# The third corner's sum moves from VectorE to TensorE, and one scan product from GpSimd to VectorE

## The chip, the cores and the metric

The kernel runs on one core of a Trainium2 chip. The core has TensorE (PE: matmuls and transposes, with its weight loads shown apart as PEld), VectorE (DVE), ScalarE (ACT), GpSimd (POOL) and the DMA queues, of which SP issues most and POOL issues the indirect ones. Each engine works through its own instructions in order; the engines wait for one another by semaphores. The metric is the device time of one execution in microseconds (us), lower is better.

## The reference, cut to what matters

Four layers run one after another on a (4, 128, 128, 128) tensor, each as `x = x + layer(groupnorm(x))`. Layer 0 is a deformable 3x3 convolution: an ordinary convolution gives each output pixel and each of nine taps an offset and a mask, the input is sampled there between its four neighbours, and the samples are projected by the weights.

```python
return corner(y0i, x0i, (1 - ly) * (1 - lx)) + corner(y0i, x0i + 1, (1 - ly) * lx) + corner(y0i + 1, x0i, ly * (1 - lx)) + corner(y0i + 1, x0i + 1, ly * lx)
...
sampled = _bilinear_sample(x, py, px) * mask[:, None]
return jnp.einsum('bckhw,ock->bohw', sampled, weight.reshape(weight.shape[0], C, KK))
```

Layer 1 is a dilated 5x7 convolution with two small projections. Layer 2 is a state-space block: after projections and a depthwise convolution, a scan with 16 states for each of 128 channels runs over the 16,384 pixels in four directions,

```python
h = h * dA + (d * u)[..., None] * b[:, :, None, :]
y = jnp.einsum('bkcn,bkn->bkc', h, c)
```

and a norm, a gate and a projection follow. Layer 3 is a 3x3 convolution with an edge term. The edit concerns the sum of the four corners in layer 0 and the products `h * c` of layer 2.

## The kernel before, in words

**Order.** The scan of layer 2 is the main line: `scan` goes through 4 images x 4 directions x 32 pieces = 512 blocks `t` of 512 pixels. All other work (the layers before and after the scan, for the images next and before) is woven in by generators: after every scan instruction `scan` yields the share of its work that is done, and `together` pulls the side work until its own share has caught up. `keep_order` at the end holds each engine to the order in which the instructions were recorded, so nothing is moved by a scheduler: an instruction that waits holds back all that stands behind it on its engine. Layer 0 of image 0 runs before the scan begins; those of images 1 to 3 run beside the scan of the image before.

**A scan block** handles 2048 rows (128 channels x 16 states) in four groups `g` of four 128x512 pieces `ng`. For each group DVE multiplies the inputs by `b` (L946, 128x2048, one factor read from PSUM); ACT makes the decays in PSUM (L875); DVE runs four scans (L989, 1.27 us each); ACT copies the last column of two pieces out as the next block's start (`carry_on`, L909); then `outputs` multiplies those two pieces in place by `c` (L915, 128x1024, both factors in SBUF): half 0 after the second scan, half 1 in the group after. PE adds the rows up with a gather matrix (`sums`, L889). A block so has eight products. While layer 0 is beside the scan (`beside["busy"] == "POOL"`, so `on_vector`), half 1's four run on DVE and half 0's four on POOL; elsewhere all are on POOL, and with `busy == "PE"` POOL also adds two pieces (L917), which saves PE a matmul. The lines around the third scan of a group:

```python
if ng == 2 and before[0] >= 0 and on_vector:
    outputs(*before, 1, nc.vector)
if ng == 2:
    carry_on(t, g, 0)
    outputs(t, g, 0)
```

**Layer 0** does 288 iterations `n` an image: 32 blocks of four rows x nine taps. `gather` (L419) issues four indirect DMAs from POOL, each of which brings, for 128 pixels, the four neighbours (128 channels each) side by side into `g`, [128, 4 rows, 4 neighbours, 128], a ring of four buffers. `weigh_low` (L433) scales neighbours 0, 1 and 2 on ACT, 128x128 at a time: neighbour 0 into the PSUM tile `pw` (bank 2), 1 and 2 in place in `g`. `weigh` on DVE adds 1 and 2 onto `pw` (L445, two 128x512 adds) and then multiplies neighbour 3 by its weight and adds `pw` in one instruction for each row (L448), which gives `v`. `turn` transposes the four rows of `v` on PE into the PSUM tile `pst` (bank 1, L456); `copy` brings it to SBUF on ACT (L460); `project` multiplies it by the tap's weights on PE (L466), which add up in bank 0 over nine taps; `add` (L473, L474) finishes a block on DVE. `positions` (from L341) makes the next strip's indices and weights in small pieces between. The iterations are laid over each other by `weave`, each step with its lag in iterations:

```python
order = [[(2, weigh_low(1)), (3, turn)], [(5, add), (0, gather), (2, weigh_low(2))],
         [(2, weigh_low(0))], [(3, copy), (0, look)], [(2, weigh), (4, project)]]
```

So in one round of the loop ACT weighs iteration n, PE turns n - 1 (whose `v` DVE made at the end of the round before), ACT copies it, DVE weighs n, PE projects n - 2, and POOL gathers n + 2. The gather takes over the buffer of four iterations before.

Of the kernel before, what the change touches and what calls it, by code (L numbers as in the profile page):

```python
# [18 lines left out]
P = 128  # L19
# [12 lines left out]
NG = 4  # L32
# [78 lines left out]
def conv_preact_kernel(ctx: ExitStack, tc: tile.TileContext, a: dict, nb: int):  # L111
    nc = tc.nc
# [11 lines left out]
    def load(pool, src, shape, name, **kw):  # L124
        t = pool.tile(shape, F32, name=name, **kw)
        nc.sync.dma_start(t, src)
        return t

    def bank(which, name):
        return psb.tile([P, N], F32, name=name, tag=f"bank{which}")  # L130
# [23 lines left out]
    ident = const.tile([P, P], F32, name="ident")  # L154
# [29 lines left out]
    for k in range(NDIR):  # L184
        pw = bank(0, "pwd")
# [8 lines left out]
    def blk(t, i):  # L194
        return t[:, i * N : (i + 1) * N]
# [99 lines left out]
    def layer0(st):  # L295
# [3 lines left out]
        with ExitStack() as s:  # L299
# [30 lines left out]
            got = {}  # L330
# [76 lines left out]
            def where(n):  # L407
                i, k = divmod(n, KK)
                return i, k, i // BPS, i % BPS
# [29 lines left out]

            def weigh(n):  # L440
                i, k, j, q = where(n)
                wv, g = got["i", j][0], got.pop(("g", n))
                pw = got.pop(("w", n)).rearrange("p (r c) -> p r c", r=R)
                for c in (1, 2):
                    nc.vector.tensor_add(pw, pw, g[:, :, c, :])  # L445
                got["v", n] = v = gp.tile([P, R, P], F32, name="v", bufs=2)
                for r in range(R):
                    nc.vector.scalar_tensor_tensor(  # L448
                        v[:, r, :], g[:, r, 3, :], wv[:, r, q, k, 3:4], pw[:, r, :], ALU.mult, ALU.add
                    )  # L450

            def turn(n):
                v = got.pop(("v", n))
                got["t", n] = pst = bank(1, "pst")
                for r in range(R):
                    nc.tensor.transpose(pst[:, r * P : (r + 1) * P], v[:, r, :], ident)  # L456

            def copy(n):
                got["c", n] = smp = pp.tile([P, N], F32, name="smp")
# [307 lines left out]
    def scan(pull):  # L767
# [11 lines left out]
        def decays(at):  # L779

            while ahead["made"] < min(at + (2 if beside.get("spare") else 1) + 1, len(seq) * NST):
                decay(ahead["made"])
                ahead["made"] += 1

        def fetch(t):
            if t < len(seq):
                st, k, i, _ = seq[t]
                while st.get("out", 0) < (i + 1 if k == 0 else NBLK + 1):
                    pull()
                    tick()  # L790
                if "y" not in st:
                    st["y"] = image("yrow"), image("ycol")
                us = st["u"]
                if not stored(us[0]):
                    flush()
                blocks[t]["u"] = load(sp, blk(us[k % 2], i), [P, N], "u", bufs=2)
# [47 lines left out]
        def spread_steps(t, g):  # L844

            blocks[t]["p", g] = p = sp.tile([P, 2, N], F32, name="spread", bufs=3)
            src = blocks[t]["steps"][g * Q : (g + 1) * Q]
            nc.sync.dma_start(
                p.rearrange("p j t -> p (j t)"), src.unsqueeze(1).to_broadcast([Q, P // Q, 2 * N])
            )  # L850
# [6 lines left out]
        def spread_states(t, what):  # L857

            blocks[t][what] = p = bp.tile([P, NG, N], F32, name=what)
            src = blocks[t]["bc"][("bb", "cb").index(what)].rearrange("(s n) t -> s (n t)", n=NG)  # L860
            nc.sync.dma_start(
                p.rearrange("p n t -> p (n t)"), src.unsqueeze(0).to_broadcast([Q, P // Q, NG * N])
            )
# [14 lines left out]
        def sums(t, g, half):  # L878

            c = blocks[t]  # L880
            second = seq[t][3]
            if g == 0 and half == 0:
                c["y"] = pss.tile([P, N], F32, name="yacc")
            last = g == NG - 1 and half == 1
            parts = (2 * half, 2 * half + 1)
            if half and c.get(("added", g)):
                parts = parts[:1]
            for ng in parts:
                nc.tensor.matmul(  # L889
                    c["y"], gather[:, g, :], c["h", g][:, ng, :],  # L890
                    start=g == 0 and ng == 0, stop=last and ng == parts[-1] and not second,
                )
            if last and second:
                nc.tensor.matmul(c["y"], ident, c["before"], start=False, stop=True)
# [9 lines left out]
        def carry_on(t, g, half):  # L904

            end = 0 if seq[t][3] else N - 1
            n = g * NG + 2 * half
            h = blocks[t]["h", g][:, 2 * half : 2 * half + 2, :]
            nc.scalar.copy(blocks[t]["carry"][:, n : n + 2].unsqueeze(2), h[:, :, end : end + 1])  # L909

        def outputs(t, g, half, engine=nc.gpsimd):

            c = blocks[t]
            h = c["h", g][:, 2 * half : 2 * half + 2, :]
            engine.tensor_mul(h, h, c["cb"][:, 2 * half : 2 * half + 2, :])  # L915
            if half and g % 2 and beside.get("busy") == "PE":
                engine.tensor_add(h[:, 0, :], h[:, 0, :], h[:, 1, :])  # L917
                c["added", g] = True
# [15 lines left out]
        for t, (st, k, i, back) in enumerate(seq):  # L934
            c = blocks[t]
            carry = c["carry"]
            more = prepare(t + 2) if t + 2 < len(seq) else iter(())
            if t > 0:
                fetch(t + 3)
            for g in range(NG):  # L940
                then = (t, g + 1) if g + 1 < NG else (t + 1, 0)
                soon = (t, g + 2) if g + 2 < NG else (t + 1, g + 2 - NG)
                before = (t, g - 1) if g else (t - 1, NG - 1)
                earlier = (t, g - 2) if g > 1 else (t - 1, g + NG - 2)
                c["h", g] = h = hp.tile([P, NG, N], F32, name="h")
                nc.vector.tensor_tensor(  # L946
                    h, c["pdu", g].unsqueeze(1).to_broadcast([P, NG, N]), c["bb"], ALU.mult
                )
                on_vector = beside.get("busy") == "POOL"
                if before[0] >= 0:  # L950
                    carry_on(*before, 1)
                    if not on_vector:
                        outputs(*before, 1)
                if soon[0] < len(seq):
                    spread_steps(*soon)
                at = t * NST + g * NG
                decays(at)
                if g == 1:
                    if t + 1 < len(seq):
                        spread_states(t + 1, "bb")  # L960
                if g == 2 and t + 1 < len(seq):
                    spread_states(t + 1, "cb")
                if g == 3 and back:
                    c["before"] = load(sp, blk(st["y"][k % 2], i), [P, N], "before")
                for ng in range(NG):
                    n = g * NG + ng
                    if ng == 1:
                        decays(at + 1)
                        if earlier[0] >= 0:
                            sums(*earlier, 1)  # L970
                    if ng == 2 and g == 1 and t > 0:
                        finish(t - 1)
                    if n % NST and ng != 2:
                        next(more, None)
                    if ng == 2 and before[0] >= 0 and on_vector:
                        outputs(*before, 1, nc.vector)
                    if ng == 2:
                        carry_on(t, g, 0)
                        outputs(t, g, 0)
                        decays(at + 2)  # L980
                        next(more, None)
                        if then[0] < len(seq):
                            inputs_up(*then)
                    if ng == 3 and before[0] >= 0:
                        sums(*before, 0)
                    o, f = h[:, ng, :], c["a", n]
                    if back:
                        o, f = o[:, ::-1], f[:, ::-1]
                    nc.vector.tensor_tensor_scan(o, f, o, carry[:, n : n + 1], ALU.mult, ALU.add)  # L989
                    if ng == 3:  # L990
                        decays(at + 3)
                    yield (t * NST + n + 1) / slots
            for _ in more:
                pass
        t = len(seq) - 1
# [396 lines left out]
```

## Time and profile before

| | |
|---|---|
| median of three runs | 22988.54 us (22963.23 to 22989.79) |
| the profiled execution's own time | 22958.5 us |
| its span, first to last instruction | 22956.7 us |
| mean granted TensorE clock | 0.872 |
| busy share of the span | PE 74%, DVE 82%, ACT 72%, POOL 75% |
| instructions | 176948 |

How to read it: a row of a group names the line, engine, operation, tiles (out<-in), shapes and count, then the busy time in us and the mean of one in ns, and then how long the engine had stood idle before such instructions and whose end released it ("issue": nothing that the profile shows). The table of stretches cuts the span by time and gives each engine's busy time in each. The granted clock is the share of full TensorE speed that the chip allowed. A busy engine is not by itself the bound; what counts is which wait ends last.

Four stretches have layer 0 in them, by the first and last gather: 236 to 2108 us, 3786 to 5873, 9486 to 11465 and 14824 to 16800. Most of the page's later slices show DVE at 8 or 9 tenths.

### The profile page before, as it was taken

The numbers are of one execution on the slowest core, as the hardware profiler recorded it, in microseconds if no ns is written. First come the engines' busy times: TensorE is split into PE (matmuls) and PEld (weight loads), VectorE is DVE, ScalarE is ACT, GpSimd is POOL, SyncE is SP. The second block draws the span as 40 slices with busy tenths as digits, with TensorE's granted clock in tenths as the row PEclk, the third lists the DMA queues.
The fourth block names the chain that finished last, engine by engine and source line by source line (L and its number), as shares of the span: only waits on it lengthen the run. The fifth ranks groups of instructions, "written<-read, shape, count | busy, mean of one in ns | idle before, by whom it ended". The sixth has DMA issues, their size and how long they took to land. (4 is left out here: it accounts for less than half of the span.)

```text
span 22956.7 us, 176948 instructions
## 1 busy us (share of the span) xinstructions
PE 16964.7 (74%) x38018; PEld 6618.0 (29%) x38018; DVE 18925.7 (82%) x19765; ACT 16485.0 (72%) x37282; POOL 17224.0 (75%) x11499
## 2 busy tenths in 40 slices
PE   3445886666878888766688887766688978788778
PEld 1112222222323333222233333322232333233223
DVE  3443489999998899889898899988898889999873
ACT  4665677888778766788868776688877867666553
POOL 3553477877788888777778788877778889877773
PEclk7667998887999999887799999987799999899889
DMA  7556468776766787777776687777776677555663
GB/s 214 175 176 182 150 204 286 249 236 227 249 204 210 216 242 258 237 238 239 240 243 203 205 251 243 248 235 244 238 254 204 206 214 231 188 196 199 194 182 111
DMA packets 2560065, 5005.19 MB, mean 218 GB/s; under 512 B 1059136, under 2 KB 1330952, under 8 KB 2416656
## 3 DMA queue, kind: packets, MB, share of 16 engines
q1 hardware_dynamic: 2190352, 3785.61, 50.8%
q0 software_dynamic: 368640, 1208.25, 17.2%
q8 instruction: 309, 5.06, 0.1%
q14 instruction: 764, 6.26, 0.1%
HBM read 4065.12 MB, written 857.74 MB: 214 GB/s over the span
## 5 line engine op out<-in xcount | busy, mean ns | idle before, releaser
L915 POOL TENSOR_TENSOR h<-h,cb 128x1024 f32<-128x1024 f32 x3740 | 8813.7, 2363 | 2826.7 <-ACT carry L909 2720.0
L989 DVE TENSOR_TENSOR_SCAN h<-pa,carry,h 128x512 f32<-128x512 f32 x8192 | 9981.1, 1267 | 277.7 <-ACT pa L875 184.0
L889 PE MATMUL yacc<-h,gather_sb 128*128 128x512 f32 x15258 | 8309.4, 675 | 1203.8 <-POOL h L915 610.9
L875 ACT ACTIVATE pa<-spread,neg_a 128x512 f32<-128x512 f32 x8192 | 5614.5, 686 | 3236.9 <-DVE h L989 3092.0
L419 POOL DMA_INDIRECT g<-table,idx x4608 | 4550.4, 988 | 2040.2 <-issue 1250.8
L946 DVE TENSOR_TENSOR h<-dub,bb 128x2048 f32<-128x2048 f32 x2048 | 4665.4, 2278 | 1297.3 <-issue 648.2
L889 PEld LDWEIGHTS yacc<-h,gather_sb 128*128 128x128 f32 x15258 | 3138.1, 217 | 5564.2 <-issue 3906.8
L456 PE MATMUL pst<-ident,v 128*128 128x128 f32 x4608 | 1193.7, 372 | 3102.3 <-DVE v L448 1666.8
L433 ACT ACTIVATE g<-g,wt 128x128 f32<-128x128 f32 x9216 | 2865.2, 389 | 171.4 <-DMA g<-table,idx 119.9
L445 DVE TENSOR_TENSOR pw<-pw,g 128x512 f32<-128x512 f32 x2304 | 1598.4, 694 | 1435.4 <-ACT pw L433 1191.6
L433 ACT ACTIVATE pw<-g,wt 128x128 f32<-128x128 f32 x4608 | 1694.9, 368 | 752.6 <-remote 298.4
L456 PEld LDWEIGHTS pst<-ident,v 128*128 128x128 f32 x4608 | 722.9, 160 | 4457.7 <-issue 2475.0
L466 PE MATMUL acc<-smp,w_sb 128*128 128x512 f32 x2304 | 1563.8, 768 | 118.7 <-DVE x L473 102.0
L448 DVE SCALAR_TENSOR_TENSOR v<-g,wt,pw 128x128 f32<-128x128 f32 x4608 | 1293.5, 342 | 114.4 <-issue 2.7
L909 ACT COPY carry<-h 128x2 f32<-128x2 f32 x4096 | 764.1, 187 | 704.2 <-DVE h L989 695.3
L855 ACT COPY dub<-spread 128x512 f32<-128x512 f32 x2048 | 1187.0, 580 | 57.3 <-DMA spread<-stepsd 19.9
L1207 PE MATMUL p<-xn,w_l_sb 128*128 128x508 f32 (+2 forms) x2304 | 1146.1, 616 | 1.8 <-ACT xn L1186 1.8
L808 PE MATMUL pdt<-u,wd 128*128 128x512 f32 x1024 | 593.4, 663 | 472.9 <-DVE h L946 431.7
L824 PE MATMUL pxbc<-u,xbc_sb 128*128 128x512 f32 x1024 | 584.8, 654 | 410.0 <-DVE h L946 406.0
L706 PE MATMUL px<-win,convw_sb 128*128 128x508 f32 (+1 forms) x1536 | 837.6, 627 | 4.7 <-DMA win<-win 4.7
L708 PE MATMUL py<-win,diag 128*64 128x508 f32 (+1 forms) x1536 | 837.0, 627 | 0.0
L460 ACT COPY smp<-pst 128x512 f32<-128x512 f32 x1152 | 664.6, 577 | 169.2 <-remote 157.1
(172 smaller groups left out, 17159.0 us busy)
## 6 DMA issues: line engine op xcount, KB each, us to landing
spread<-stepsd SPq DMA_DIRECT2D x2048, 512.0 KB
bb<-bcd SPq DMA_DIRECT2D x512, 1024.0 KB
cb<-bcd SPq DMA_DIRECT2D x512, 1024.0 KB
stepsd<-steps SPq DMA_DIRECT2D x512, 512.0 KB
table<-gt SPq DMA_DIRECT2D x512, 256.0 KB
g<-table,idx POOLq DMA_INDIRECT x4608
u<-urow SPq DMA_DIRECT2D x256, 256.0 KB
yrow<-y SPq DMA_DIRECT2D x256, 256.0 KB
```

What stands on the lines that cost most here:

```text
L419: nc.gpsimd.indirect_dma_start(out=g[:, r].rearrange("p q c -> p (q c)"), out_offset=None, in_=table, in_offset=bass.IndirectOffsetOnAxis( ...
L433: nc.scalar.activation(pw[:, r * P : (r + 1) * P] if c == 0 else g[:, r, c, :], g[:, r, c, :], AF.Copy, scale=wv[:, r, q, k, c : c + 1],)
L445: nc.vector.tensor_add(pw, pw, g[:, :, c, :])
L448: nc.vector.scalar_tensor_tensor(v[:, r, :], g[:, r, 3, :], wv[:, r, q, k, 3:4], pw[:, r, :], ALU.mult, ALU.add)
L456: nc.tensor.transpose(pst[:, r * P : (r + 1) * P], v[:, r, :], ident)
L466: nc.tensor.matmul(got["a", i], w0[:, k, :], got.pop(("c", n)), start=k == 0, stop=k == KK - 1)
L855: nc.scalar.copy(p, blocks[t]["p", g][:, 1, :])
L875: nc.scalar.activation(pa, blocks[t]["p", g][:, 0, :], AF.Exp, scale=neg_a[:, k, n : n + 1])
L889: nc.tensor.matmul(c["y"], gather[:, g, :], c["h", g][:, ng, :], start=g == 0 and ng == 0, stop=last and ng == parts[-1] and not second,)
L915: engine.tensor_mul(h, h, c["cb"][:, 2 * half : 2 * half + 2, :])
L946: nc.vector.tensor_tensor(h, c["pdu", g].unsqueeze(1).to_broadcast([P, NG, N]), c["bb"], ALU.mult)
L989: nc.vector.tensor_tensor_scan(o, f, o, carry[:, n : n + 1], ALU.mult, ALU.add)
```

## The change

`weigh` adds only neighbour 1 on DVE. Neighbour 2, weighed by ACT as before, is now added by PE: `turn` makes each row's transpose as two matmuls with the identity into the same PSUM columns, one of neighbour 2's weighed rows and one of `v`. They are ordinary f32 matmuls, no longer transposes. The buffer `g` is so read by PE last, and is given back after `turn` instead of after `weigh`. In `scan`, where layer 0 is beside it, half 0's product of the last group goes to DVE too: five of eight on DVE, three on POOL. Nothing else is changed; the lines after L445 move by one or two.

```diff
             def weigh(n):
                 i, k, j, q = where(n)
-                wv, g = got["i", j][0], got.pop(("g", n))
+                wv, g = got["i", j][0], got["g", n]
                 pw = got.pop(("w", n)).rearrange("p (r c) -> p r c", r=R)
-                for c in (1, 2):
-                    nc.vector.tensor_add(pw, pw, g[:, :, c, :])
+                nc.vector.tensor_add(pw, pw, g[:, :, 1, :])
...
             def turn(n):
-                v = got.pop(("v", n))
+
+                v, g = got.pop(("v", n)), got.pop(("g", n))
                 got["t", n] = pst = bank(1, "pst")
                 for r in range(R):
-                    nc.tensor.transpose(pst[:, r * P : (r + 1) * P], v[:, r, :], ident)
+                    dst = pst[:, r * P : (r + 1) * P]
+                    nc.tensor.matmul(dst, g[:, r, 2, :], ident, start=True, stop=False)
+                    nc.tensor.matmul(dst, v[:, r, :], ident, start=False, stop=True)
...
                     if ng == 2:
                         carry_on(t, g, 0)
-                        outputs(t, g, 0)
+                        outputs(t, g, 0, nc.vector if on_vector and g == NG - 1 else nc.gpsimd)
```

## The prediction

> **What bounds the kernel now.** I began with the page. Its first part names VectorE (DVE), busy for 82% of the span, above GpSimd (POOL, 75%), TensorE (PE, 74%) and ScalarE (ACT, 72%); but no engine is full, and the shares mix stages. Line 419 (the gathers) is issued only while the deformable layer runs, and its times divide the span: A (240 to 2110 us, the layer of image 0, alone) and B, C, D (the layers of images 1 to 3, each woven into the scan of another image). The edit touches only these. The table of stretches is next; its columns are length, busy us and count of PE, PE's weight loads, DVE, ACT and POOL, then PE's granted clock, DMA share and GB/s. The last two rows are stretches without the layer.
>
> ```profile
> 240.00:2110.00 1870.00, 830.95 (x2232) 315.27 (x2232) 822.74 (x2004) 1223.80 (x3732) 1087.41 (x1149) 0.64 0.59 174
> 3800.00:5890.00 2090.00, 1353.51 (x3399) 553.76 (x3400) 1956.05 (x2783) 1788.54 (x4892) 1631.52 (x1398) 0.81 0.73 237
> 9500.00:11478.00 1978.00, 1267.79 (x3238) 529.24 (x3238) 1752.75 (x2663) 1705.50 (x4715) 1540.66 (x1360) 0.79 0.73 239
> 14838.00:16814.00 1976.00, 1261.54 (x3238) 524.21 (x3238) 1747.85 (x2664) 1705.01 (x4716) 1541.80 (x1360) 0.79 0.74 239
> 6750.00:7750.00 1000.00, 893.71 (x1845) 309.42 (x1843) 861.07 (x610) 815.42 (x1506) 826.82 (x455) 0.97 0.64 208
> 22000.00:22500.00 500.00, 377.19 (x682) 139.39 (x682) 359.22 (x263) 287.51 (x560) 359.07 (x202) 0.88 0.61 183
> ```
>
> DVE fills 94% of B and 89% of C and D, ACT 86%. DVE is the nearest to a bound, with ACT close behind. The groups of DVE in C (line, operation, shape, count | busy us, mean ns | idle before, by whom ended) show what it does for the layer, and that its idle time is waiting for ACT's weighing:
>
> ```profile
> L445 DVE TENSOR_TENSOR pw<-pw,g 128x512 f32<-128x512 f32 x575 | 398.3, 693 | 177.8 <-ACT pw L433 143.2 <-DMA g<-table,idx 13.9 <-issue 10.7
> ...
> L915 DVE TENSOR_TENSOR h<-h,cb 128x1024 f32<-128x1024 f32 x108 | 178.6, 1653 | 0.0
> ```
>
> How much of a DVE microsecond reaches the end? The scan's blocks (16 scans each) have different DVE loads, so I cut B, C and D at the first scan of each block, in the same table of stretches. A light and a heavy block of C, and the sum of its 25:
>
> ```profile
> 10541.50:10624.80 83.30, 48.30 (x111) 21.01 (x109) 74.34 (x118) 66.08 (x183) 61.98 (x57) 0.75 0.70 224
> ...
> 11290.50:11358.70 68.20, 41.36 (x96) 17.90 (x96) 59.43 (x87) 61.03 (x169) 55.24 (x49) 0.78 0.76 249
> ...
> sum 1840.30, PE 1178.69 PEld 494.71 DVE 1634.71 ACT 1583.12 POOL 1430.81; mean PE 47.15 PEld 19.79 DVE 65.39 ACT 63.32 POOL 57.23
> ```
>
> A line through the 25 blocks of C gives 0.62 us of block for each us of DVE, through the 26 of D 0.61; the lighter against the heavier halves give 0.54 and 0.56. I take 0.58. B's 29 blocks give 0.78. A mean block is 65.7 us with 9 iterations in B, and 73.5 with 10.7 in C and D: 32 blocks in B and 27 each in C and D for 288 iterations.
>
> **Part 1: DVE loses one add.** One L445 of 0.694 us goes in each iteration: 6.25 us a block in B, 7.4 in C and D.
>
> **Part 2: DVE gains a product.** In each block beside the layer, the product of group 3, first half, moves from POOL to DVE: 89 in all (DVE has 356 at four a block). Undisturbed it takes 1.22 us. In the timeline of C (start, length) it can take longer:
>
> ```profile
> 10314.78 2.39 POOL L915 TENSOR_TENSOR h<-h,cb 128x1024 f32<-128x1024 f32 x1
> ...
> 10315.44 2.81 DVE L915 TENSOR_TENSOR h<-h,cb 128x1024 f32<-128x1024 f32 x1
> ```
>
> DVE's product ends 1.1 us after POOL's, as if it could start only then; every long one in the records has another POOL elementwise operation beside it. The POOL product in this fence is the very one that is moved, so its victim, the DVE product of group 2 just before, loses that wait: at group 3 the records give a mean of 1.71, so 0.49 us comes back. The Trainium skill, SBUF — State Buffer, "Who interferes with whom", states that a VectorE instruction with both inputs in SBUF and a GpSimd one that reads SBUF block each other for the whole instruction, which speaks against giving DVE such a product; by it alone each new one could wait out another POOL operation, 89 × 1.6 = 142 us of DVE time, and the sum below would lose some 90 us. The row shows the block, and also that the usual culprit here goes.
>
> The product also gets a wait: it overwrites the rows that ACT's carry copy (L909) reads. Behind it on DVE stand the third scan and all that follows. In the records that copy ends before DVE would be free in three of four blocks, late otherwise; the mean wait is 0.55 us (bounds: 0, and 1.8, the lateness that one block of ten in C exceeds). Net on DVE per block: B −6.25 + 1.22 + 0.55 − 0.5 = −5.0; C and D −7.4 + 1.22 + 0.55 − 0.49 = −6.1. On the path: B 32 × 5.0 × 0.78 = 125; C and D 54 × 6.1 × 0.58 = 191. **Together −316 us.** POOL's 89 × 2.4 us freed count nothing: it is idle for 22% of these stretches. PE's 27,648 more instructions (12 × 1152, each with a weight load) cost nothing to load: instruction queues take 0.2% of the DMA time.
>
> **Part 3: PE's turn grows.** Four transposes were four instructions; now eight matmuls. The records show each ordinary f32 matmul as two instructions, so the turn has 16. No turn of this kind is in the trace; the nearest rows are the old one at both clocks:
>
> ```profile
> 10200.59 1.16 PE L456 MATMUL pst<-ident,v 128*128 128x128 f32 x4 [4.38 <-issue]
> ...
> 10206.99 0.60 PE L456 MATMUL pst<-ident,v 128*128 128x128 f32 x4
> ```
>
> Less the last one's length (0.46 and 0.27) that is 0.23 apart at half clock and 0.11 at full. (The 128-column edge matmuls of L1207 start 0.11 to 0.19 apart at full clock; the first is taken, as the weight loads are 0.11 apart in both.) So 16 take 1.8 to 3.7 us, where four took 0.44 to 0.92. Does PE have room? At full clock a 512-column instruction takes 0.43 (four L889 in 1.88, less the last's excess). C then needs (2086 × 0.43 + 1152 × 0.11) / 1978 = 0.52 of its time, and is granted 0.79. In the two rows without the layer the same sum gives 0.59 at 0.88 and 0.79 at 0.97. With the new turns C needs (2086 × 0.43 + 288 × 16 × 0.11) / 1880 = 0.75, so I expect some 0.95: room is left, the old matmuls get faster, and a turn step takes about 0.15 on the mean, as it begins after idle.
>
> The Trainium skill, TensorE: Matmul & The Clock Gate, Part 1, says the array runs at half clock until some 3.4 us of sustained work, and Part 4 that transposes don't count as such work. By Part 1 a turn after a pause would run at half clock to its end, and the sum would be that of the slower rival below; by Part 4 the exchange itself warms the array. The rows above bear on load and clock, not on the first microseconds of a burst.
>
> Who waits for the turn: ACT's copy (L460), with all of ACT's weighing behind it. From the first finished piece of v, 14 instructions are left: 13 × 0.15 + 0.3 = 2.3 us, against 1.0 now, so 1.3 later; v itself comes up to 0.69 earlier. I take a delay of 1.0. In the records the copy starts 1.02 us after the turn at the earliest, 2.4 at the median of C and 3.1 of B. Laid against these, 1.0 makes the copy wait 0.22 us an iteration in C and D and 0.16 in B (a delay of 2.0: 0.72 and 0.53). With the same shares as above: 576 × 0.22 × 0.58 + 288 × 0.16 × 0.78 = **+109 us**.
>
> **Part 4: the gather buffer is held longer.** The turn now reads g, so a gather waits for PE's turn four iterations back, not for DVE. In B to D the gather starts 7 us after that at the median: free. In A it is tight (timeline):
>
> ```profile
> 1207.76 1.12 DVE L448 SCALAR_TENSOR_TENSOR v<-g,wt,pw 128x128 f32<-128x128 f32 x4
> ...
> 1208.26 1.16 PE L456 MATMUL pst<-ident,v 128*128 128x128 f32 x4 [0.66 <-DVE v L448]
> ...
> 1209.62 0.94 POOL L419 DMA_INDIRECT g<-table,idx  x1 [8.30 <-ACT pw L433]
> ```
>
> POOL starts 0.74 us after DVE's last piece, having idled 8.3. A goes in cycles of five iterations: 20 gathers of 1.25 us, then such an idle. The release moves by 12 × 0.16 − 0.63 (the turn starts before the last piece) − 0.69 = +0.6 a cycle; 58 cycles: **+35 us**. Bounds: nothing (A's ACT stalls hide it), or 1.4 us in each iteration, the lengthened ring through the copy at half clock: +400.
>
> **Sum.** −316 + 109 + 35 = −172. The profiled execution took 22958.5 (span 22956.7, and 1.8 around it), so 22786.5; the median of the three runs is 30 above it, so I forecast 22,817, or 0.75% faster. What this measurement can tell from no change is about 0.2%, 46 us.
>
> **Rivals.** (a) *All of DVE's saving arrives*: share 1, no copy wait: 32 × 5.0 + 54 × 6.1 = 489, so 22,500. For it: 94% in B. Against: ACT has 63.3 us in a 73.5 us block and DVE falls to 59, so ACT bounds next. (b) *ACT is the bound already in C and D*: only B's 125 arrive, and the copy's 109 and A's 35 use them up: 22,990 to 23,010, no change. (c) *Slower: the cold turn takes the add's place.* If each burst runs at half clock, 14 instructions take 3.5 us, the copy comes 2.05 to 2.45 later and waits 0.74 to 1.0 us in C and D and 0.55 to 0.75 in B: 371 to 503 us; A adds 58 × 1.4 = 81. Against −316 that is +136 to +268: 23,125 to 23,255. It decides from a step of some 0.20 us, where the copy's waits eat the 281 left after A. For it: four of five turns in C are cold now. Against: the load and clock rows. (d) *The change does less than it says*: the fifth product goes to DVE only while the layer runs, 89 of 512 blocks; this is counted above.
>
> **Numbers.** Forecast's case 0.52, (a) 0.13, (b) 0.12, (c) 0.23. Faster by over 0.2%: 0.65; within: 0.12; slower: 0.23. The range leaves out the far half of (a) and (c): 22,520 to 23,140.
>
> **What would show it.** L445 at 1152, DVE's products at 445, POOL's at 3651; DVE's busy share in C at 86 to 88%; PE's clock there at 0.9 or more, turn steps near 0.15; ACT's copy with a little idle before it, ended by the turn; B some 90 us shorter, C and D some 60 each, A equal or slightly longer. A clock still near 0.8 with ACT idle at the copy would make me wrong towards (c); DVE's idle time grown by all that was saved, towards (b).

## The result, and the profile after

The changed kernel takes 22,986.88 us (median of 12 runs, 22,968.94 to 23,009.46), the kernel before 22,985.28 us (12 runs, 22,963.23 to 23,017.05). The ratio is 0.9999, with a 95% interval of 0.9991 to 1.0007: **no change**, where 0.75% faster was forecast. The profiled execution of the changed kernel has a span of 22,998.3 us, 42 more than that of before, with 204,063 instructions and a mean granted clock of 0.905.

The first view is the table of stretches, cut from the first gather to the last piece of `v` (columns as in the prediction: length, then busy us and count of PE, PE's weight loads, DVE, ACT and POOL, then clock, DMA share, GB/s). The first four rows are the kernel before, cut in the same way, the last four the changed kernel.

```profile
236.20:2120.40 1884.20, 836.62 (x2246) 317.46 (x2246) 829.40 (x2021) 1232.51 (x3757) 1090.41 (x1152) 0.64 0.58 173
3785.80:5890.80 2105.00, 1363.49 (x3416) 555.95 (x3415) 1970.44 (x2800) 1799.34 (x4918) 1644.12 (x1409) 0.81 0.73 237
9485.50:11478.60 1993.10, 1271.90 (x3244) 530.68 (x3244) 1764.51 (x2677) 1713.28 (x4735) 1552.81 (x1370) 0.79 0.73 238
14823.60:16814.40 1990.80, 1265.58 (x3244) 525.67 (x3244) 1759.07 (x2676) 1712.48 (x4735) 1553.86 (x1370) 0.79 0.74 239
...
236.80:2003.60 1766.80, 1170.41 (x5693) 845.45 (x5694) 630.99 (x1732) 1239.23 (x3757) 1092.57 (x1152) 0.81 0.63 185
3670.30:5774.50 2104.20, 1628.99 (x6863) 1000.02 (x6862) 1813.42 (x2543) 1794.17 (x4917) 1538.94 (x1377) 0.88 0.72 237
9373.10:11437.40 2064.30, 1552.01 (x6689) 976.76 (x6690) 1611.44 (x2415) 1713.05 (x4735) 1493.21 (x1343) 0.88 0.71 230
14786.70:16845.70 2059.00, 1554.20 (x6691) 977.74 (x6692) 1610.06 (x2416) 1712.56 (x4735) 1490.04 (x1343) 0.87 0.71 231
```

A is 117 us shorter, B is unchanged, C is 71 longer and D 68. The work moved as planned: DVE's busy time in C fell from 1764.5 to 1611.4 us, and ACT's did not change (1713). But DVE's share of C is 78%, not the 86 to 88% forecast. Its two groups in C (columns: count | busy us, mean ns | idle before, by whom ended) have half the adds and 27 more products, and both wait for ACT:

```profile
L917 DVE TENSOR_TENSOR h<-h,cb 128x1024 f32<-128x1024 f32 x136 | 207.5, 1531 | 60.9 <-ACT carry L911 31.7 <-ACT pw L433 12.8 <-issue 8.4
L444 DVE TENSOR_TENSOR pw<-pw,g 128x512 f32<-128x512 f32 x288 | 198.7, 690 | 295.6 <-ACT pw L433 235.7 <-DMA g<-table,idx 35.5 <-issue 21.6
```

So ACT is late. In the same view ACT's copy of the turn shows why. First the kernel before, then the changed one, both in C:

```profile
L460 ACT COPY smp<-pst 128x512 f32<-128x512 f32 x287 | 165.5, 576 | 7.8 <-remote 7.7
```

```profile
L462 ACT COPY smp<-pst 128x512 f32<-128x512 f32 x287 | 166.4, 580 | 176.8 <-remote 122.1 <-PE pst L458 14.4 <-PE acc L468 13.6
```

The copy waits 176.8 us, 0.62 an iteration where 0.22 was forecast. Only 14.4 of that ends with the turn (L458). 122.1 us are put down to "remote": the semaphore moves, but no instruction that moves it has ended in the 1.5 us before. One such wait in the timeline of the changed kernel (start, length):

```profile
10231.05 1.57 ACT L433 ACTIVATE pw<-g,wt 128x128 f32<-128x128 f32 x4
...
10232.24 0.63 PE L458 MATMUL pst<-ident,v 128*128 128x128 f32 x2
...
10235.05 1.02 PE L468 MATMUL acc<-smp,w_sb 128*128 128x512 f32 x2
10236.18 0.95 POOL L419 DMA_INDIRECT g<-table,idx  x1 [0.80 <-issue]
10237.44 0.95 POOL L419 DMA_INDIRECT g<-table,idx  x1 [0.30 <-issue]
10238.69 0.95 POOL L419 DMA_INDIRECT g<-table,idx  x1 [0.31 <-issue]
10239.72 0.59 ACT L462 COPY smp<-pst 128x512 f32<-128x512 f32 x1 [7.10 <-remote]
10239.94 0.95 POOL L419 DMA_INDIRECT g<-table,idx  x1 [0.30 <-issue]
10240.20 0.20 ACT L911 COPY carry<-h 128x2 f32<-128x2 f32 x1
...
10240.36 0.79 PE L457 MATMUL pst<-ident,g 128*128 128x128 f32 x2 [4.28 <-ACT smp L462]
10240.43 1.23 DVE L917 TENSOR_TENSOR h<-h,cb 128x1024 f32<-128x1024 f32 x1 [4.72 <-ACT carry L911]
```

The turn's last matmul ends at 10232.87 by the profile, and PE goes on to other work until 10236.07. The trace records that the semaphore moves at 10239.70, 6.8 us after the turn's end. ACT idles 7.10 us before it copies; the carry copy behind it, DVE's product and PE's next turn are all late with it. I call such waits **held news**: ACT waits over 1 us for something that has ended in the records, and the profile says "remote" (the expectations speak of held signals). The traces have 76 of them (460 us) before, nearly all in A, and 226 (792 us) after. All of them lie in the four stretches with gathers.

### The profile page after: what moved, and what is told of

Read it like the earlier page. It is cut to its first block, busy times and chain, and to the rows that moved or that the text cites. A ratio compares the mean times of both kernels' runs of the same rounds, so it can differ in the third digit from the quotient of the medians.

```text
span 22998.3 us, 204063 instructions
## 1 busy us (share of the span) xinstructions
PE 18163.5 (79%) x51842; PEld 8500.5 (37%) x51842; DVE 18272.6 (79%) x18702; ACT 16498.6 (72%) x37282; POOL 16998.6 (74%) x11410
## 5 line engine op out<-in xcount | busy, mean ns | idle before, releaser
L917 POOL TENSOR_TENSOR h<-h,cb 128x1024 f32<-128x1024 f32 x3651 | 8606.0, 2364 | 2892.7 <-ACT carry L911 2842.4
L891 PE MATMUL yacc<-h,gather_sb 128*128 128x512 f32 x15258 | 7972.1, 651 | 1218.4 <-POOL h L917 612.6
L891 PEld LDWEIGHTS yacc<-h,gather_sb 128*128 128x128 f32 x15258 | 3013.6, 209 | 5437.4 <-issue 3786.2
L457 PE MATMUL pst<-ident,g 128*128 128x128 f32 x9216 | 2197.5, 327 | 1569.0 <-ACT smp L462 1223.6
L457 PEld LDWEIGHTS pst<-ident,g 128*128 128x128 f32 x9216 | 1748.4, 231 | 2425.4 <-ACT smp L462 1724.6
L458 PE MATMUL pst<-ident,v 128*128 128x128 f32 x9216 | 2195.7, 327 | 379.2 <-DVE v L447 228.6
L444 DVE TENSOR_TENSOR pw<-pw,g 128x512 f32<-128x512 f32 x1152 | 797.9, 693 | 1875.9 <-ACT pw L433 1519.8
L458 PEld LDWEIGHTS pst<-ident,v 128*128 128x128 f32 x9216 | 1737.8, 235 | 477.8 <-DVE v L447 281.4
L468 PE MATMUL acc<-smp,w_sb 128*128 128x512 f32 x2304 | 1317.1, 656 | 93.9 <-DVE x L475 83.1
```

The lines of the kernel that those rows point to most:

```text
L457: nc.tensor.matmul(dst, g[:, r, 2, :], ident, start=True, stop=False)
L458: nc.tensor.matmul(dst, v[:, r, :], ident, start=False, stop=True)
L468: nc.tensor.matmul(got["a", i], w0[:, k, :], got.pop(("c", n)), start=k == 0, stop=k == KK - 1)
L891: nc.tensor.matmul(c["y"], gather[:, g, :], c["h", g][:, ng, :], start=g == 0 and ng == 0, stop=last and ng == parts[-1] and not second,)
```

## The experiments

The theories. *Turn*: the turn's 16 instructions make the copy late, and ACT is the bound. *Product*: the fifth product costs what the add gives. *Release*: holding `g` until the turn delays the gathers. *Held news*: what is late is not the turn but the word of it. *Chip* came later. Times are medians; ratios are to the kernel before, run beside it on the same chip. The records name the chips 5, 2 and 3. On chip 5 the kernel before takes 22,987 to 22,992 us and its trace is like the one of the result; on 2 and 3 it takes 22,505 and 22,483 to 22,485.

### Chip 5: parts of the change alone

**e1, the turn without the product**

```diff
-                        outputs(t, g, 0, nc.vector if on_vector and g == NG - 1 else nc.gpsimd)
+                        outputs(t, g, 0)
```

> The changed kernel with the fifth product given back to POOL (DVE has four in a block, as before); the longer turn stays. Turn theory (ACT's copy waits for the longer turn, and since ACT is the bound in C and D this wait eats what DVE saves): the product hardly matters, so A is some 117 us shorter than before, B about equal, C and D some 50 to 80 us longer each, and the whole within 22,900 to 23,030. Product theory (the fifth product, which waits for ACT's carry copy and holds up the third scan, gives the saving back): C and D come out 60 to 120 us shorter than before each, B 90 or more, and the whole 22,450 to 22,650.

Measured: 22,987.15, ratio 1.0001 (0.9991 to 1.0010); stretches 1768, 2107, 2061 and 2067. On this chip the product costs the changed kernel nothing that can be measured: the product theory falls.

**e2, the product without the turn** (the reverse edit in the kernel before)

> The kernel before with the fifth product given to DVE and the old turn. Turn theory: DVE pays 1.22 + 0.55 - 0.5 = 1.27 us a block, of which 0.78 (B) or 0.58 (C, D) reaches the end: 32 x 1.27 x 0.78 + 54 x 1.27 x 0.58 = 72, so about 23,055, with A as before. Product theory: it has to account for what went missing, some 300 us or more: 23,280 or longer.

Measured: 23,332.62, ratio 1.0153 (1.0139 to 1.0167). That is +345 us, a time that the product theory allows, but the extra time goes with something else: B, C and D are 100, 120 and 143 longer, and held news of 99, 122 and 137 us is there now, with the old turn (0, 11 and 9 in the kernel before). Groups of ACT in C:

```profile
L433 ACT ACTIVATE pw<-g,wt 128x128 f32<-128x128 f32 x1152 | 423.9, 368 | 191.6 <-remote 65.8 <-DVE v L448 43.6 <-issue 30.0
L460 ACT COPY smp<-pst 128x512 f32<-128x512 f32 x287 | 165.5, 577 | 59.8 <-remote 51.2 <-issue 8.6
```

In the first row ACT waits for an earlier instruction of its own, which has ended: all 113 held waits of this group in e2's trace are on ACT's own semaphore. So it is not PE's news alone that is held. This kernel was run on chip 5 only, so what the product costs without held news is not measured.

**e3, DVE's relief alone**

```diff
-                for c in (1, 2):
-                    nc.vector.tensor_add(pw, pw, g[:, :, c, :])
+                nc.vector.tensor_add(pw, pw, g[:, :, 1, :])
```

> The kernel before with DVE's second add left out and nothing in its place: neighbour 2 does not enter the sum (ACT still weighs it). This is DVE's relief alone, with the old turn and four products. If my shares were right: B 32 x 6.25 x 0.78 = 156 shorter, C and D 27 x 7.4 x 0.58 = 116 each, and A perhaps 117 as in the changed kernel: 22,480 to 22,600. If ACT is already the bound in C and D (rival b of the prediction): C and D unchanged, B 100 to 156 shorter, A up to 117: 22,710 to 22,885.

Measured: 22,771.77, ratio 0.9910 (0.9895 to 0.9926): −215. A is 58 shorter, B 71, C 39, D 33. My shares would have made it 156, 116 and 116 in B to D. The whole lies in the range of the second theory, but C and D do get shorter, so ACT is not simply their bound; and the share of DVE's time that arrives is less than half of what I took.

**e4, the turn's cost alone**

```diff
-                    nc.tensor.transpose(pst[:, r * P : (r + 1) * P], v[:, r, :], ident)
+                    dst = pst[:, r * P : (r + 1) * P]
+                    nc.tensor.matmul(dst, zero[:, 0:P], ident, start=True, stop=False)
+                    nc.tensor.matmul(dst, v[:, r, :], ident, start=False, stop=True)
```

> The kernel before, both adds on DVE and four products, but the turn made as long as the changed one: for each piece a matmul of a tile of zeros and then one of v, 16 TensorE instructions; it does not read g, so the gather's buffer is released by DVE as before. This is the turn's cost alone, without any saving. Turn theory: ACT's copy waits some 0.5 to 0.7 us an iteration beside the scan, so C and D get 100 to 200 us longer each, B 50 to 150, and the whole 23,250 to 23,450. Release theory (what costs is that the gather's buffer g is held by the turn): no change, 22,940 to 23,030.

Measured: 23,604.39, ratio 1.0274 (1.0260 to 1.0288): +617, more than either allowed. A alone is 270 longer. Its copy in A and in C:

```profile
L462 ACT COPY smp<-pst 128x512 f32<-128x512 f32 x287 | 167.4, 583 | 878.6 <-remote 855.0 <-PE pst L458 13.5 <-PE acc L468 7.2
```

```profile
L462 ACT COPY smp<-pst 128x512 f32<-128x512 f32 x287 | 166.3, 579 | 210.5 <-remote 120.7 <-PE pst L458 23.3 <-issue 21.7
```

As the main cause the release theory falls, since `g` is released early here. Of the turn's price, the part that ends with the turn itself is again small (23.3 us in C).

### Chip 2: buffers, a later copy, and a surprise

**e5, three gather buffers** (`bufs=4` to `bufs=3` in the changed kernel)

> The changed kernel with three gather buffers instead of four, so POOL can't issue as many gathers in a row. Held-signal theory (what ACT's copy waits for in the changed kernel is not the turn's work but news of it, which comes only some 2 us after the last gather of a burst): bursts get shorter, the copy's waits that nothing in the profile ends fall to under half of the 122 us in C and D, and C and D come to 1,950 to 2,010 us each (2,064 and 2,059 in the changed kernel). Release theory (the buffer that the turn holds is what is missing): gathers come later still, C and D 2,120 us or more each, the whole over 23,100. A is open in both: shorter bursts against a tighter ring.

Measured: 22,527.00, ratio 1.0009 (1.0000 to 1.0018). The opposite, five buffers (e6), has no time: one pool of the kernel needs 11.3 kb a partition, and five buffers leave it 6.1.

**e7, the copy a little later** (in the changed kernel)

```diff
-            order = [[(2, weigh_low(1)), (3, turn)], [(5, add), (0, gather), (2, weigh_low(2))],
-                     [(2, weigh_low(0))], [(3, copy), (0, look)], [(2, weigh), (4, project)]]
+            order = [[(4, copy), (2, weigh_low(1)), (3, turn)], [(5, add), (0, gather), (2, weigh_low(2))],
+                     [(2, weigh_low(0))], [(0, look)], [(2, weigh), (4, project)]]
```

> The changed kernel with ACT's copy moved from the end of its round to the start of the next (the turn before it in program order, the project after it, as now), so that the turn has some 2 us more before ACT asks for it. Turn theory (its 2.2 us of work instead of 1.0): the copy's waits vanish, C and D come to 1,940 to 1,960, B to 2,020 to 2,060, the whole 22,750 to 22,830. Held-signal theory: the waits last 3 to 6 us each, so 2 us of slack takes off a third to a half: C and D 1,990 to 2,040, the whole 22,850 to 22,950.

Measured: 22,289.96, ratio 0.9906 (0.9891 to 0.9921).

**e8, v by ordinary matmuls** (8 instructions in the kernel before)

```diff
-                    nc.tensor.transpose(pst[:, r * P : (r + 1) * P], v[:, r, :], ident)
+                    nc.tensor.matmul(pst[:, r * P : (r + 1) * P], v[:, r, :], ident, start=True, stop=True)
```

> The kernel before with the four transposes of v as four ordinary matmuls of v against the identity: 8 TensorE instructions instead of 4, still four signals. Turn theory in proportion to work (16 instructions cost 617 us in the run with a tile of zeros): about a third, 23,150 to 23,250. If the number of signals is what counts: no change, 22,950 to 23,030. Held-signal theory: waits that nothing in the profile ends show in B to D where the kernel before had hardly any, as far as the time goes up at all.

Measured: 22,522.87, ratio 1.0010 (1.0001 to 1.0019), +18 us.

None of the three can be laid against chip 5's runs: the kernel before takes 482 us less here, and not one of these traces has held news, e8's included, whose layer 0 is almost the kernel before's. So the held news might belong to the chip and not to the kernel.

### Chip 5 again

**e9, the kernel before**

> The kernel before, unchanged, for its trace. The runs of the three buffers, the late copy and the v matmuls were made on another chip than all earlier ones: the kernel before took 22,505 us there, 482 less, and not one ACT wait over 1 us that nothing in the profile ends shows in those three traces. Chip theory (such waits are a trait of the chip, not of the kernel): if this run is on a chip where the kernel before takes about 22,505, the trace shows A near 1,450 us (1,885 on the first chip), B to D within 30 us of 2,105, 1,993 and 1,991, and no such waits; if it takes about 22,985, the trace of before repeats.

Measured: 23,006.65 in one run; stretches 1882, 2114, 2011 and 2000, held news of 417 us in A. The first trace repeats.

**e10, the changed kernel**

> The changed kernel, unchanged. Chip theory: where the kernel before takes about 22,505, there are no such waits, the copy's waits come from the turn alone, and my sum should hold: 0.7 to 0.9% faster than before (22,305 to 22,350), C and D about 1,935 each and B 2,015. Turn theory: no change there either, 22,480 to 22,530. Where the kernel before takes about 22,985, no change again in both.

Measured: 22,983.65, ratio 0.9996 (0.9987 to 1.0005).

**e11, the later copy**

> The changed kernel with ACT's copy at the start of the next round. Where the kernel before takes about 22,505: 0.94% faster again, and if the changed kernel as it is does as well, the later copy adds nothing to it. Where it takes about 22,985: turn theory, 22,750 to 22,830; held-signal theory, 22,850 to 22,950, as the waits last longer than the slack given.

Measured: 22,920.08, ratio 0.9968 (0.9955 to 0.9980), in the range of the held-news theory. Its reason does not show, though: held waits were to fall by a third to a half, and they sum to 753 us where e10's trace has 773. The copy in C waits less, and its waits for nothing shown stay:

```profile
L462 ACT COPY smp<-pst 128x512 f32<-128x512 f32 x287 | 165.5, 577 | 131.2 <-remote 100.2 <-PE acc L468 20.2 <-PE pxbc L826 4.7
```

The same kernel had no held news on chip 2 and 134 such waits in A alone here. Of the kernels that leave nothing out this is the fastest on chip 5; elsewhere its ratio (0.9906 on chip 2) is that of the changed kernel (0.9911 on chip 3, e13).

**e12, the turn with zeros**

> The kernel before with the turn lengthened by matmuls of zeros (it cost 617 us on the first chip: 270 of it in A, 68 in B, 129 in C, 156 in D). Chip theory, where the kernel before takes about 22,505: only the copy's waits for real work remain, which I priced at 109 us in the prediction, so 22,560 to 22,650. Turn theory: 22,800 or more there too.

Measured: 23,629.95, ratio 1.0276 (1.0262 to 1.0290): e4 repeats.

### Chip 3: the change where nothing is held

**e13, the changed kernel**

> The changed kernel, unchanged. Where the kernel before takes about 22,505 us: no waits of ACT that nothing in the profile ends, and by the terms of my sum 22,305 to 22,350; by the turn theory 22,480 to 22,530. Where the kernel before takes about 22,985: no change again.

Measured: 22,279.48, ratio **0.9911** (0.9897 to 0.9924), 204 us less than before, and 26 us below the range that my sum gave. The turn theory falls. The stretches:

```profile
236.10:1685.50 1449.40, 1085.19 (x5693) 727.25 (x5694) 629.40 (x1733) 1250.37 (x3757) 1090.74 (x1152) 0.90 0.76 225
3349.80:5372.00 2022.20, 1596.38 (x6864) 984.15 (x6863) 1819.05 (x2544) 1793.98 (x4918) 1543.93 (x1377) 0.90 0.75 247
8961.20:10879.30 1918.10, 1508.51 (x6691) 947.77 (x6692) 1611.93 (x2416) 1707.87 (x4735) 1493.37 (x1343) 0.89 0.77 248
14223.20:16134.40 1911.20, 1509.94 (x6691) 954.38 (x6692) 1608.95 (x2416) 1708.51 (x4735) 1494.77 (x1343) 0.90 0.77 249
```

**e17, the kernel before, for its trace**

> The kernel before, unchanged, for its trace. Where it takes about 22,490 us (no held signals): A near 1,450, B near 2,110, C and D near 1,985, so that the changed kernel's 2,022, 1,918 and 1,911 there are 60 to 90 us shorter each, as forecast. Where it takes about 22,985: the first trace repeats.

Measured: 22,500.92 in one run. Its stretches:

```profile
236.10:1689.20 1453.10, 837.94 (x2246) 314.73 (x2246) 830.84 (x2020) 1247.38 (x3757) 1093.08 (x1152) 0.67 0.75 225
3355.70:5463.60 2107.90, 1361.75 (x3416) 557.61 (x3415) 1968.24 (x2800) 1799.34 (x4918) 1646.61 (x1409) 0.82 0.73 237
9065.40:11041.70 1976.30, 1269.46 (x3244) 526.54 (x3244) 1771.81 (x2676) 1711.60 (x4735) 1558.52 (x1370) 0.79 0.75 240
14388.00:16365.80 1977.80, 1268.24 (x3244) 528.60 (x3244) 1772.20 (x2676) 1712.38 (x4735) 1558.04 (x1370) 0.79 0.75 240
```

Here the change takes 4 us off A, 86 off B, 58 off C and 67 off D. In B to D the engines' busy times are those of chip 5 to about 3%; what is gone is idle time. The copy in C, before and then after:

```profile
L460 ACT COPY smp<-pst 128x512 f32<-128x512 f32 x287 | 165.4, 576 | 0.0
```

```profile
L462 ACT COPY smp<-pst 128x512 f32<-128x512 f32 x287 | 165.6, 577 | 18.1 <-PE pst L458 17.8
```

So ACT waits 18.1 us in C for the longer turn itself, and 17.8 of it is ended by the turn.

**e14 and e18, three gather buffers, twice more**

> The changed kernel with three gather buffers instead of four. Where the kernel before takes about 22,985 us, held-signal theory: POOL can run ahead by a gather group less, bursts get shorter than 8 in A and 12 beside the scan, and ACT's waits that nothing in the profile ends fall to less than half (467 us in A, 122 in C and in D), the whole 22,600 to 22,900; if bursts have nothing to do with it, the waits stay as many and the whole is 23,000 or more. Where the kernel before takes about 22,505: 22,527 again.

> The changed kernel with three gather buffers. Where the kernel before takes about 22,985 us: if bursts of gathers hold the news, ACT's waits that nothing in the profile ends fall to less than half (467 us in A, 122 in C and in D), the whole 22,600 to 22,900; if bursts have nothing to do with it, they stay, and the whole is 23,000 or more. Where the kernel before takes about 22,490: 22,520 again.

Measured: 22,516.62, ratio 1.0016 (1.0006 to 1.0025), and 22,525.85, ratio 1.0017 (1.0008 to 1.0026). With nothing held, a buffer less costs the changed kernel some 240 us: A 1528.5, C 1988.1 (e18). ACT's weighing then waits for the gathers themselves, 164.6 us in C where the change alone has 80 (and the kernel before 57.6):

```profile
L433 ACT ACTIVATE g<-g,wt 128x128 f32<-128x128 f32 x2304 | 733.9, 390 | 166.0 <-DMA g<-table,idx 164.6
```

So at four buffers the turn's hold on `g` costs ACT some 22 us of waiting in C, and one buffer less is where it would be paid. What shorter bursts do on chip 5 was not tried: both runs went to chip 3.

**e15, e16 and e19, plain loads in place of the gathers**

```diff
-                    nc.gpsimd.indirect_dma_start(
-                        out=g[:, r].rearrange("p q c -> p (q c)"),
...
-                    )
+                    nc.sync.dma_start(g[:, r].rearrange("p q c -> p (q c)"), table[m % 128 * P : (m % 128 + 1) * P])
```

> The changed kernel with POOL's indirect gathers left out: g is filled by SyncE with plain loads of the same size from fixed rows of the table (so the samples are those of wrong places). Held-signal theory (POOL's gathers hold the news): on any chip no waits of ACT that nothing in the profile ends, and this kernel is 150 to 230 us faster than the kernel before with the same plain loads, as in my sum. If the waits come from the DMA traffic or from the chip alone, they stay where the kernel before takes about 22,985, and the two kernels with plain loads differ by less than 60 us.

> The kernel before with the same plain loads by SyncE in place of POOL's gathers (samples of wrong places): the control for the changed kernel with plain loads. Held-signal theory: no such waits, 150 to 230 us slower than that one; otherwise within 60 us of it.

> The changed kernel with plain loads by SyncE in place of POOL's gathers (samples of wrong places). Where the kernel before takes about 22,985 us: if the gathers hold the news, there are no waits of ACT that nothing in the profile ends and the time is that of the other chip, 21,780 to 21,830; if it is the chip's DMA traffic whoever issues it, the waits are there and the time is 22,000 or more. Where the kernel before takes about 22,490: 21,798 again.

Measured: changed 21,798.14 (ratio 0.9696, 0.9682 to 0.9709) and again 21,807.61 (0.9699, 0.9685 to 0.9713), before 22,129.59 (0.9843, 0.9830 to 0.9857). The change is worth 331 us here, more than the 150 to 230 expected: without POOL's gathers B shortens by 97 us, C by 115 and D by 109. No news is held, but on chip 3 it is not held with the gathers either, so this does not show that the gathers hold it.

## Why the prediction was wrong, step by step

**Where the saving went.** The change's own effect, read on chip 3, is −4 − 86 − 58 − 67 = −215 us. On the result's chip the kernel before is longer than there by 431 us in A, −3 in B, 17 in C and 13 in D, 458 together. Its held waits sum to 440, 0, 11 and 9 us, 460 together. The changed kernel is longer by 317, 82, 146 and 148, 693 together; its held waits sum to 467, 83, 121 and 121, 792 together. So the change brings 235 us more of such loss, and −215 + 235 = +20. That sum holds by the way it is made; what bears it out is that the held waits, counted for themselves, match the loss to within 30 us in seven of the eight stretches. In the eighth, A of the changed kernel, they are 150 us more than the loss, and there ACT waits 157 us less for the gathers than on chip 3 (16.5 against 173.6).

**The step that failed** is in Part 3: "In the records the copy starts 1.02 us after the turn at the earliest", and the delay of 1.0 us laid against those margins. It took for granted that ACT learns of the turn about a microsecond after its end. (1.02 is the tenth percentile in C; the earliest is 0.80.) On the result's chip the word sometimes comes 3 to 7 us late, and with the changed kernel far more often beside the scan (C: 122.1 us of the copy's waits against 7.7). The page of before did not lack the sign: in A, where ACT waits for itself or for PE, I named "A's ACT stalls" and used them as cover, without asking what ended them. These are their rows:

```profile
L433 ACT ACTIVATE pw<-g,wt 128x128 f32<-128x128 f32 x1152 | 423.7, 368 | 477.8 <-remote 296.8 <-ACT pw L433 102.9 <-issue 52.2
L460 ACT COPY smp<-pst 128x512 f32<-128x512 f32 x287 | 165.9, 578 | 148.1 <-remote 143.9 <-issue 4.2
```

The other steps:

- *Part 1, the add.* It went as counted. Its worth was oversized: e3 gives 143 us in B to D where the shares 0.78 and 0.58 make 388. A slope over light and heavy blocks mixes in whatever else makes a block heavy. That e3 was measured among held news leaves the add's size on the other chips open.
- *Part 2, the product.* In the changed kernel it costs nothing on chip 5 (e1). Its wait for the carry copy is 38.4 us in C on chip 3, 1.4 a block instead of 0.55; DVE has room for it there, as it waits 219.7 us for its add. In the kernel before it cost 345 us on chip 5 (e2) where my terms make 72, and the held waits grew by 338 us in B to D. So the two halves of the change are no sum there. What the product costs where nothing is held is not shown.
- *Part 3, the turn.* Its arithmetic was right: 0.15 us a step, 2.2 us from the first matmul of `v` to the end (2.3 forecast). The clock in C is 0.88, not 0.95. With nothing held the copy waits 18.1 / 287 = 0.06 us an iteration, not 0.22, so by the same shares the turn costs about a third of the 109 us (an estimate).
- *Part 4, the release.* A was to grow by 35; it changes by −4 on chip 3 and by −117 on the result's chip. There POOL issues its gathers in runs of eight where the kernel before has 16 to 20, which fits with PE letting it go one iteration at a time. That the shorter runs are the cause is argued, not shown.
- *The sum.* On chip 3 the forecast case holds: 172 forecast, 204 measured, B −86 of −90, C and D −58 and −67 of −60, and DVE fills 84% of C where 86 to 88 was forecast. Part of that is luck: B to D together change by −211, and with about 34 us for the turn (an estimate from the copy's waits there, 13.9, 18.1 and 21.9 us, by my shares) the saving is some 245 where I had 316. Saving and price were both too large, and their errors cancel. The changed kernel was not run on chip 2.
- *The rivals.* (b) has the result's time, not its reason: "ACT is the bound already in C and D" would hold on every chip, and C gets 58 us shorter on chip 3. (c)'s cold turn did not come. I had no rival for news that is late.

**Still open**: what holds the news on chip 5. In A of the changed kernel the middle half of the held waits end 1.8 to 1.9 us after the last gather of a run (138 waits), which points to POOL's gathers; in C some end while gathers go on, as in the timeline above.

The trace's list of semaphore moves points the same way. In the result's trace 46% of the instructions of PE, ACT and DVE that move a semaphore in the four stretches (13,486 of 29,205) have no move on record within 0.08 us of their end; outside the stretches not one of 33,740 lacks it, and on chip 3 ten of 29,205 do in the stretches. The share is 14% in the first 3 us of a run of gathers, 81% from 8 us on, and none of 2,267 later than 3 us after its end. So on chip 5 the trouble comes and goes with the runs of gathers. A missing record is not yet a late word (81 of C's 287 copies in the kernel before start ahead of the next move on record), and the same gathers hold nothing on chips 2 and 3. Why they do on chip 5 stays open, as the runs without gathers, or with shorter runs of them, fell on a chip where nothing is held.

The Trainium skill, Perfetto Trace Analysis, "Tensor Engine Instruction (MATMUL, LD_WEIGHTS)", says that the end shown for a matmul is worked out from its size, and that its semaphore moves only when PSUM has acknowledged the write. So the trace can't tell a turn whose word is late from one that really ended late; ACT's 113 held waits for itself in e2 speak for the word being late, since the modelled ends are PE's.

## What to carry to other kernels

Before pricing a change by the margins of a trace, look at every wait that nothing in the profile ends: a stall that is unexplained before the change will not stay where it was when engines are re-timed. Price the parts of a change together (on chip 5 the product cost 345 us without the freed add, nothing with it), and don't read the worth of an engine's microsecond off a slope of busy against length. When a result contradicts a sum and the trace shows waits that nothing ends, run both kernels on another chip before looking for the error in the sum.

## What the runs showed of the hardware

- Three chips gave two behaviours for one program: the kernel before takes 22,987 us on chip 5, 22,505 on chip 2 and 22,483 on chip 3, with 431 us of the difference between chips 5 and 3 in stretch A, which is the layer alone (1884 against 1453 us). On chips 2 and 3 no trace has a single held wait.
- In e4's stretch A on chip 5 the copy's held waits sum to 855 us, and the longest is 15.4 us; in one of 12.7 us PE, DVE and ACT all stand idle for the last 10, and POOL's gathers go on until 2.4 us before its end.
- The Trainium skill, SBUF — State Buffer, "Who interferes with whom", states that PE and ACT never wait on anyone. No run here shows ACT waiting for a port; but the sentence does not cover ACT's 113 waits in e2 on its own semaphore, for instructions that had ended.
- More work on PE went with a higher clock: in C on chip 3 PE's instructions rose from 3244 to 6691, its busy time from 1269 to 1509 us, and the granted clock from 0.79 to 0.89.
